# A graph-network kernel: the last 23 supertiles' messages are kept in DRAM, three slot tables serve in turn, and the turning of messages, the first fills and the last bins are done differently

## The chip, the cores and the metric

The kernel runs on one core of a Trainium2 chip. The metric is the device time of one execution in microseconds (us). The kernel before took 4111.01 us (median of three runs, 4106.05 to 4113.0).

## The reference

A message-passing layer over 12,500 nodes (128 features each) and 400,000 edges sorted by `dst`:

```python
h = jnp.maximum(_layernorm(x, axis=-1), 0.0)
# layer: f_ij = edge_attr_20 (400000 x 20), rcut = edge_weight, idx_i = src (random), idx_j = dst (sorted)
h = h @ W_in2f.T
Wij = smu(f_ij @ W_f1.T + b_f1) @ W_f2.T + b_f2
Wij = Wij * rcut_ij[:, None]
x_ij = h[idx_j] * Wij
agg = jax.ops.segment_sum(x_ij, idx_i, num_segments=h.shape[0])
out = smu(agg @ W_o1.T + b_o1) @ W_o2.T + b_o2
return x + out
```

`smu` is a smooth leaky unit; the kernel builds it from a Gelu and a linear part.

## The kernel before

**Tiles.** A tile is 128 edges. There are 3125 tiles; four make a group (782 groups), eight make a supertile (391, the last one short). The nodes fall into 98 bins of 128.

**One group.** Because `dst` is sorted, the rows of `h` that a group needs lie in one window of 42 rows. For each group the kernel makes on TensorE (PE), VectorE (DVE) and ScalarE (ACT): `hide` (L563, first filter product `pu`), `bend` (L571, Gelu), `smooth` (L579, DVE), `weigh` (L616, second product `pw`), `gather` (L597, one-hot product that picks the rows of `h`), `take` (L605), `mix` (L626, DVE: product with the rows of `h`, giving `mt`), `turn` (L636: `mt` becomes rows by edge and is multiplied by `w_o1` in the same four fp32 matmuls), `send` (L643, L646: ACT scales the rows by the edge weight into a buffer `ms`, six of which exist, with the place within the bin in column 128). Beside that, `bins`, `count`, `read` and `number` (L497, L511 to L514, L541, L550) give each edge a slot in its bin.

**The scatter.** Since `src` is random, `send` does not add. It issues, on GpSimd's (POOL's) queue, one indirect DMA for each tile (L649) that writes 128 rows of 129 floats to their slots in a table in DRAM.

**Epochs.** The edges are cut into nine epochs of 59, 59, 59, 59, 48, 37, 27, 27 and 16 supertiles (`PARTS`). Each has a table `buf` of its own with `CAP` slots a bin (768 down to 256, so Q = 6, 6, 6, 6, 5, 4, 3, 3, 2 blocks of 128). Slots that may stay empty are zeroed first (`clear`, on SP's queue). While epoch k is computed, the table of epoch k-1 is read back (`fetch`, L680, SP's queue, chunks of up to 12 blocks) and summed: `choose` (L691, DVE) makes one-hot selections `se` from column 128, `add` (L704, PE) does one matmul for each bin and block, and DVE adds four bins at a time into `agg` (L715, L717). `chores` of that kind start four groups after an epoch's first (`WAIT`).

**Order.** PE, DVE, ACT and SP run the order in which the program issues (`manual_schedule`); the main loop over `g` writes it out by hand and reaches up to three groups ahead.

**The ends.** Before the first scatter DVE converts the first indices (L305, `whole_bins`) and builds constants while POOL fills buffers with memsets (L291, L404). After the last scatter the table of the last epoch is summed and the output is made in 26 units of up to four bins: Gelu (L994, ACT), `sm` (L1000, POOL), product with `w_o2` (L264, PE), addition of the old rows of `x` (L268, DVE), store (L270). The old rows get the output bias on POOL (L250, `with_bias`), 12 of the 26 units' rows while the last epoch is scattered.

Of the kernel before, what the change touches and what calls it, by code (L numbers as in the profile page):

```python
# [19 lines left out]
P = 128  # L20
# [11 lines left out]
PARTS = (59, 59, 59, 59, 48, 37, 27, 27, 16)  # L32
# [8 lines left out]
def gnn_kernel(  # L41
# [46 lines left out]
    for a, n in eps_of:  # L88
        mean = n * SUP * P * P / N
        dev = SIGMA * math.sqrt(mean)  # L90
        CAP.append(math.ceil((mean + dev) / P) * P)
        ZMIN.append(max(0, math.floor((mean - dev) / ZP) * ZP))
# [10 lines left out]
    bufs = [dram.tile([NB * CAP[k], ROW], F32, name=f"buf{k}") for k in range(EPOCHS)]  # L103
# [24 lines left out]
    nc.vector.tensor_scalar(lift, ident, BIG, None, op0=ALU.mult)  # L128
    nc.vector.scalar_tensor_tensor(tri, irow, pcol, lift, op0=ALU.is_gt, op1=ALU.add)
    ones_h = const.tile([P, P], F16, name="ones_h")  # L130
    nc.vector.memset(ones_h, 1.0)
    rest_h = const.tile([P, P], F16, name="rest_h")
    nc.vector.tensor_sub(rest_h, ones_h, tri)
    none = const.tile([P, NB], F16, name="none")
    nc.vector.memset(none, 0.0)
# [6 lines left out]
    b1w = const.tile([P, P], F32, name="b1w")  # L142
# [14 lines left out]
    b2row = const.tile([1, P], F32, name="b2row")  # L157
    b1 = const.tile([P, 1], F32, name="b1")
    bz = const.tile([P, 1], F32, name="bz")
    w_o1 = const.tile([P, P], F32, name="w_o1")  # L160
# [4 lines left out]
    zero = const.tile([ZP, CB * max(c - z for c, z in zip(CAP, ZMIN)) * ROW // ZP], F32, name="zero")  # L165
# [69 lines left out]
    units = [(b, n, P) for b, n in chunks(NB - 1, GRP)] + [(NB - 1, 1, LASTB)]  # L235
# [39 lines left out]
    with tc.tile_pool(name="ld", bufs=4) as ld, \  # L275
# [8 lines left out]
        irow_ps = ps1.tile([P, GRP * P], F32, name="irow_ps")[:, 0:P]  # L284
        nc.vector.tensor_copy(irow_ps, irow)
# [106 lines left out]
        fill(0, nc.vector)  # L392
        nc.gpsimd.memset(w_f1, 0.0)
        nc.gpsimd.dma_start(w_f1[0:R, :], w_f1_t)
        nc.gpsimd.dma_start(w_f1[R:R + 1, :], b_f1)
        nc.sync.dma_start(fbufs[0][0:R, :], f_t[:, 0:SUP * P])
        nc.scalar.dma_start(w_o1, w_o1_t)
        nc.scalar.dma_start(x_sb[:, 1:HEAD, :], bin_rows(x, 1, HEAD - 1))
        nc.gpsimd.dma_start(w_f2, w_f2_t)
        nc.gpsimd.dma_start(b2, b_f2.rearrange("o p -> p o"))  # L400
        one["fetched"]()
        nc.gpsimd.dma_start(w_sb[:, 0:CH], w_col[:, 0:CH])
        fill(1, nc.gpsimd)
        nc.gpsimd.memset(zero, 0.0)  # L404
        clear(0, len(cleans) - 1, nc.gpsimd)
        fill(2, nc.gpsimd)
        zr = edge.tile([P, 3 * D], BF, name="zr", bufs=1)
        nc.gpsimd.memset(zr, 0.0)
        nc.gpsimd.dma_start(h_dram[NB * P:N + P, :], zr[:N + P - NB * P, :])
        fill(3, nc.gpsimd)  # L410
        nc.gpsimd.memset(x_sb[:, NB - 1, :], 0.0)
# [11 lines left out]
        def last_loads():  # L423
            nc.sync.dma_start(b2row, b_f2)
            nc.sync.dma_start(bo2, b_o2.to_broadcast([P, P]))

        groups = [(t0 + a, g) for t0, nt in sups for a, g in chunks(nt, GRP)]
        epoch = [k for k, (a, n) in enumerate(eps_of) for _ in range(n)]
# [3 lines left out]
        def load(s):  # L432
            if s >= NS:
                return
            t0, nt = sups[s]
            e0, n = t0 * P, nt * P
            fb = fbufs[s % NF]
            if s > 0:
                nc.sync.dma_start(fb[0:R, :n], f_t[:, e0:e0 + n])
            loaded[s] = (fb,)  # L440
            if s > 2:
                targets(s)

        def targets(s):
# [3 lines left out]
            rb = ld.tile([P, SUP * P], BF, name="rbc")  # L448
# [28 lines left out]

        def tiles_of(k):
# [3 lines left out]
        def bins(g):  # L482
# [5 lines left out]
            so = cnt.tile([P, GRP, NB], F16, name="so")  # L488
            if g in first:
                k = first[g]  # L490
                m = FEW if g == 0 else tiles_of(k)
                begins[k] = (t, cnt.tile([P, max(n for _, n in eps_of) * SUP], F32, name="hic", bufs=2))
                nc.vector.tensor_scalar(begins[k][1][:, :m], hi_f[:, t:t + m], float(CAP[k]), -BIG, op0=ALU.mult, op1=ALU.add)
                last[0] = none
            before = last[0]
# [3 lines left out]
            last[0] = so[:, n - 1]  # L499
# [44 lines left out]
        def number(g):  # L544
# [4 lines left out]
            ix = cnt.tile([P, GRP], I32, name="ix", bufs=8)  # L549
# [80 lines left out]
        def turn(g):  # L630
# [4 lines left out]
            for j in range(n):  # L635
                nc.tensor.matmul(pt[:, j, :], mt[:, j * P:(j + 1) * P], w_o1, start=True, stop=True)  # L636
            mixed[g] = pt

        def send(g):
# [3 lines left out]
            nc.scalar.activation(ms[:, :n, P], lo_b[:, t:t + n], AF.Copy)  # L643
            pt = mixed.pop(g)
            for j in range(n):
                nc.scalar.activation(ms[:, j, 0:P], pt[:, j], AF.Copy, scale=w_sb[:, t + j:t + j + 1])  # L646
            k, ix = epoch[g // PER], taken.pop(g)
# [36 lines left out]
        def choose(k, c):  # L684

            if c is None:
# [4 lines left out]
            nc.vector.tensor_tensor(se[:, :m], irow_ps.unsqueeze(1).to_broadcast([P, m, P]),  # L691
                                    rows_in[c][:, :m, P:P + 1].to_broadcast([P, m, P]), op=ALU.is_equal)
            sel[c] = se

        def add(k, b, q):

            g = b % GRP
            c, i = b // SPAN[k], b % SPAN[k]
            if q == 0 and g == 0:
# [11 lines left out]
            if g == GRP - 1 or b == NB - 1:  # L711
# [4 lines left out]
                else:  # L716
                    nc.vector.tensor_add(dst, dst, src)  # L717

# [15 lines left out]
        def homes():  # L734
            spent = eps_of[-1][0] * SUP // (GRP * P) * (GRP * P)
            for t in (w_sb, hi_f):
                for o in range(0, spent, GRP * P):
                    yield t[:, o:o + GRP * P]
            for o in range(0, spent // 2 // (GRP * P) * (GRP * P), GRP * P):
                yield lo_w.bitcast(F32)[:, o:o + GRP * P]  # L740

        held = {unit: home.rearrange("p (b d) -> p b d", b=GRP)
                for unit, home in zip([u for u in units if u[1] == GRP][::2], homes())}
        ahead = list(held)
# [26 lines left out]
        stats(edge, 0)  # L771
        few = edge.tile([FEW, P], BF, name="few", bufs=1)
# [3 lines left out]
        deviations(0, 1)  # L776
# [16 lines left out]
        product()  # L793
        bins(0)
        for s in (1, 2):
            load(s)
# [12 lines left out]
        for s in (1, 2):  # L809
            targets(s)  # L810
# [19 lines left out]
        def output_bias():  # L830

            nc.vector.tensor_scalar(w_o2, w_o2, GC, None, op0=ALU.mult)
            nc.vector.tensor_scalar(bz, b1, ZS, None, op0=ALU.mult)
            nc.vector.tensor_scalar(b1w, onesb, b1, LIN, op0=ALU.mult, op1=ALU.mult)
            pb1 = bank("pb1")[:, 0, :]
            nc.tensor.matmul(pb1, b1w, w_o2, start=True, stop=True)
# [64 lines left out]
        for g in range(NG):  # L901
            s = g // PER
            k = epoch[s]
            g0, ng = eps_of[k][0] * PER, min(eps_of[k][1] * PER, NG - eps_of[k][0] * PER)
            i = g - g0
            if g == (FEW // SUP - 3) * PER:
                assert not opening
            if g % PER == 0:
                load(s + 3)
# [7 lines left out]
            elif k + 1 < EPOCHS:  # L917
# [5 lines left out]
            if k and i == 0:  # L923
                work = [(b, q) for b in range(NB) for q in range(Q[k - 1])]
# [5 lines left out]
            if k and k == EPOCHS - 1 and i >= WAIT and ahead:  # L930
                unit = ahead.pop(0)
                old_rows(unit, held[unit], nc.sync)
            lo = hi = 0
# [4 lines left out]
            if g:  # L938
# [3 lines left out]
            number(g + 1)  # L942
            weigh(g + 1)
            gather(g + 1)
            take(g + 1)
            parts(k - 1, lo + (hi - lo) // 2)
            mix(g + 1)
            step()
            hide(g + 2)
            bend(g + 2)  # L950
            count(g + 2)
            smooth(g + 2)
            if g % PER == 0:
                pick((g + 4) // PER)
            bins(g + 3)
# [238 lines left out]
```

## Time and profile before

| What | us |
|---|---|
| median of three runs | 4111.01 |
| profiled execution, its own time | 4114.52 |
| span of its trace | 4112.7 |
| busy: PE, DVE, POOL, ACT | 3675.1, 3450.5, 3096.4, 1944.9 |
| first and last scatter start (L649) | 19.9, 4022.2 |
| mean granted TensorE clock | 0.976 |

The span runs from the first instruction to the last; 1.8 us of the execution's own time lie outside it. Shares of busy time are averages over the whole span. A matmul's busy time overlaps that of the next. "Idle before" names what ended an engine's wait; "issue" means that the profile shows nothing that it waited for.

### The profile page before, as it was taken

What the parts mean: (1) busy time and instruction counts of PE and PEld (TensorE: products, weight loads), DVE (VectorE), ACT (ScalarE), POOL (GpSimd) and SP (SyncE); (2) the same over time, 40 slices, a digit from 0 to 9 for tenths busy, and PEclk for the clock granted to TensorE, in tenths of its full rate; (3) what the DMA queues carried; (4) which work ended last, traced back from release to release, by engine and by line L of the source; (5) the groups of instructions that cost most, each with busy time, mean ns of one, the idle gap of its engine ahead of it and who ended that gap; (6) DMA issues with size and microseconds to landing.
All of it is one profiled execution on the core that took longest, in us unless ns stands there. A gap on an engine that the chain in (4) does not pass through costs nothing.

```text
span 4112.7 us, 74065 instructions
## 1 busy us (share of the span) xinstructions
PE 3675.1 (89%) x21113; PEld 2552.3 (62%) x21117; DVE 3450.5 (84%) x7657; ACT 1944.9 (47%) x5690; POOL 3096.4 (75%) x3199
## 2 busy tenths in 40 slices
PE   7878887999888998979999979999899989999898
PEld 4445545666655666646666656666677767666678
DVE  8988776888878888868888868888799979888897
ACT  4457754444444444435444434444444434444442
POOL 6777777777777777777777777777777777777775
PEclk9999998999999999989999989999999999999999
DMA  6866656766647666646766647777688789887668
GB/s 187 231 187 182 191 166 183 213 202 195 188 141 219 198 201 197 199 146 196 212 199 187 199 148 207 210 204 211 176 228 223 195 230 242 221 228 221 176 195 248
DMA packets 564245, 820.83 MB, mean 200 GB/s; under 512 B 178033, under 2 KB 378488, under 8 KB 563698
## 3 DMA queue, kind: packets, MB, share of 16 engines
q1 hardware_dynamic: 456096, 604.98, 53.5%
q0 software_dynamic: 100320, 207.40, 15.7%
q10 hardware_dynamic: 7410, 3.65, 0.3%
q8 instruction: 167, 2.74, 0.3%
q14 instruction: 252, 2.06, 0.2%
HBM read 442.34 MB, written 373.37 MB: 198 GB/s over the span
## 4 chain that ended last, share of the span: by engine, by line
PE 39%; DVE 29%; DMA 18%; ACT 6%; issue 5%; POOL 2%; DVEq 0%; ACTq 0%; POOLq 0%; SPq 0%
DMA buf<-ms,ix 17%; PE pt L636 11%; PE pg L704 9%; PE pw L616 8%; DVE se L691 8%; PE pu L563 7%; DVE mt L626 5%; DVE so L497 5%; DVE sm L579 3%; DVE sl L541 3%; ACT ge L571 2%; ACT ms L646 2%; PE ph L597 2%; POOL buf L649 2%; DVE agg L717 1%
## 5 line engine op out<-in xcount | busy, mean ns | idle before, releaser
L649 POOL DMA_INDIRECT buf<-ms,ix x3125 | 3025.4, 968 | 972.7 <-issue 395.9
L646 ACT ACTIVATE ms<-pt,w_sb 128x128 f32<-128x128 f32 x3125 | 888.8, 368 | 1125.5 <-PE pt L636 1118.0
L636 PE MATMUL pt<-w_o,mt 128*128 128x128 f32 x6250 | 881.3, 284 | 390.9 <-DVE mt L626 388.4
L704 PEld LDWEIGHTS pg<-se,rw 128*128 128x128 f32 x8036 | 1052.4, 192 | 249.7 <-issue 210.8
L704 PE MATMUL pg<-se,rw 128*128 128x128 f32 x8036 | 1148.8, 280 | 4.5 <-DVE se L691 3.7
L636 PEld LDWEIGHTS pt<-w_o,mt 128*128 128x128 f32 x6250 | 765.5, 193 | 478.7 <-DVE mt L626 474.5
L497 DVE SCALAR_TENSOR_TENSOR so<-irow_ps,hi_f,so 128x98 f16<-128x98 f32 x3116 | 989.0, 317 | 82.7
L616 PE MATMUL pw<-sm,w_f 128*128 128x512 f32 x1564 | 826.7, 611 | 10.4 <-DVE sm L579 8.5
L563 PE MATMUL pu<-f,w_f 128*128 128x512 f32 x1564 | 811.4, 601 | 0.0
L626 DVE SCALAR_TENSOR_TENSOR mt<-pw,b,hg 128x512 f32<-128x512 f32 x782 | 583.6, 746 | 207.3 <-ACT hg L605 203.8
L571 ACT ACTIVATE ge<-pu 128x512 f32<-128x512 f32 x782 | 468.6, 599 | 532.7 <-PE pu L563 526.5
L579 DVE SCALAR_TENSOR_TENSOR sm<-pu,ge 128x512 f32<-128x512 f32 x782 | 535.3, 684 | 187.8 <-ACT ge L571 182.0
L691 DVE TENSOR_TENSOR se<-irow_ps,rw 128x1536 f32<-128x1536 f32 (+1 forms) x345 | 587.9, 1704 | 114.3 <-DMA rw<-buf 110.2
L605 ACT ACTIVATE hg<-ph 128x512 f32<-128x512 f32 x782 | 468.6, 599 | 62.1 <-PE ph L597 44.9
L541 DVE TENSOR_REDUCE sl<-pc 128x4 f32<-128x392 f32 x782 | 434.7, 556 | 0.0
L643 ACT ACTIVATE ms<-lo_b 128x4 f32<-128x4 bf16 x782 | 159.9, 204 | 358.7 <-DMA buf<-ms,ix 358.2
L597 PE MATMUL ph<-oh,hw 126*128 126x512 bf16 x770 | 298.3, 387 | 0.0
L563 PEld LDWEIGHTS pu<-f,w_f 128*128 128x128 f32 x1564 | 253.5, 196 | 53.4 <-issue 43.8
L511 PE MATMUL pc<-so,tri 128*128 128x392 f16 x782 | 257.9, 330 | 1.0 <-DVE sl L541 0.8
L616 PEld LDWEIGHTS pw<-sm,w_f 128*128 128x128 f32 x1564 | 241.1, 195 | 24.7 <-DVE sm L579 21.4
L513 PEld LDWEIGHTS <-rest_h 128*128 128x128 f16 x781 | 76.5, 98 | 265.9 <-issue 265.9
L513 PE MATMUL pc<-so,rest_h 128*128 128x294 f16 x781 | 225.1, 288 | 0.0
(161 smaller groups left out, 1391.0 us busy)
## 6 DMA issues: line engine op xcount, KB each, us to landing
rw<-buf SPq DMA_DIRECT2D x292, 774.0 KB
rbc<-rel_dram SPq DMA_DIRECT2D x389, 256.0 KB
buf<-zero SPq DMA_DIRECT2D x243, 387.0 KB
buf<-ms,ix POOLq DMA_INDIRECT x3125
buf<-zero SPq DMA_DIRECT2D x193, 258.0 KB
rw<-buf SPq DMA_DIRECT2D x49, 645.0 KB
f<-in_f_t SPq DMA_DIRECT2D x390, 80.0 KB
hw<-h_dram SPq DMA_DIRECT2D x770, 31.5 KB
```

The lines of the kernel that those rows point to most:

```text
L497: nc.vector.scalar_tensor_tensor(so[:, j], irow_ps[:, :NB], hi_f[:, t + j:t + j + 1], so[:, j - 1] if j else before, op0=ALU.is_equal, op1 ...
L541: nc.vector.tensor_reduce(sl[:, :n], pc[:, :n], op=ALU.max, axis=AX.X)
L563: nc.tensor.matmul(pu[:, :n], w_f1, loaded[g // PER][0][:, o:o + n], start=True, stop=True)
L571: nc.scalar.activation(ge[:, :n], units_of[g][:, :n], AF.Gelu, scale=ZS)
L579: nc.vector.scalar_tensor_tensor(sm[:, :n], units_of.pop(g)[:, :n], LIN, hidden[g][:, :n], op0=ALU.mult, op1=ALU.add)
L616: nc.tensor.matmul(pw[:, :n], w_f2, hidden.pop(g)[:, :n], start=True, stop=True)
L626: nc.vector.scalar_tensor_tensor(mt[:, :n], pws.pop(g)[:, :n], b2, rows_of.pop(g)[:, :n], op0=ALU.add, op1=ALU.mult)
L636: nc.tensor.matmul(pt[:, j, :], mt[:, j * P:(j + 1) * P], w_o1, start=True, stop=True)
L646: nc.scalar.activation(ms[:, j, 0:P], pt[:, j], AF.Copy, scale=w_sb[:, t + j:t + j + 1])
L649: i = nc.gpsimd.indirect_dma_start(out=bufs[k][:, :], out_offset=bass.IndirectOffsetOnAxis(ap=ix[:, j:j + 1], axis=0), in_=ms[:, j, :], in ...
L691: nc.vector.tensor_tensor(se[:, :m], irow_ps.unsqueeze(1).to_broadcast([P, m, P]), rows_in[c][:, :m, P:P + 1].to_broadcast([P, m, P]), op= ...
L704: nc.tensor.matmul(pgs[0][:, g, :], rows_in[c][:, o, 0:P], sel[c][:, o, :], start=(q == 0), stop=(q == Q[k] - 1))
```

## The change

Seven things are done:

1. **Ten epochs instead of nine**, with 59, 59, 59, 59, 48, 37, 27, 20, 16 and 7 supertiles; Q of the last ones is 3, 3, 2, 1. The sum of Q over all epochs goes from 41 to 42.
2. **The last two epochs (23 supertiles, from `EARLY` = 368) are computed early.** After supertile 67, 76, 85 and so on to 265 (every ninth in epochs 1 to 4) one of them is put in between: 6, 7, 6 and 4 of them in the four epochs. Their messages aren't scattered then, but written to `kept_rows` in DRAM by one DMA a group on ACT's queue; their slots are kept in `ix_kept`. After the main loop `refill` reads each group back on SP's queue, four groups ahead, and `scatter` puts it into its table.
3. **Three tables serve in turn** (`BUFS`), so only epochs 0 to 2 are cleared. A later user of a table adds 128 or more to column 128 (`mark`), and `choose` compares with a row of `irow` shifted as much (`marks`), so that what an earlier epoch left there isn't selected.
4. **`turn` transposes** (matmul with `ident` in transpose mode) for the first 368 supertiles; `w_o1` is applied once to `agg`, by 25 matmuls of up to 512 columns (`fold`), after epoch 7 has been summed. The 23 others keep the old form.
5. **POOL's first fills** come after five two-column memsets that DVE does behind the first four sums of `bins(0)`, and DVE's counting constants (`tri`, `rest_h` and others) move to just ahead of `bins(0)`. Five small loads go from POOL's queue to SP's.
6. **The bias** is added to the old rows on DVE, while the kept messages are scattered; the rows are loaded then too, into buffers that are free by that time.
7. **At the end** the first full selection of the last epoch is made in pieces of four blocks, and one output unit of four bins is cut into two of two.

```diff
-PARTS = (59, 59, 59, 59, 48, 37, 27, 27, 16)
+PARTS = (59, 59, 59, 59, 48, 37, 27, 20, 16, 7)
+SENT_LAST = 2
+BUFS = 3
...
-    bufs = [dram.tile([NB * CAP[k], ROW], F32, name=f"buf{k}") for k in range(EPOCHS)]
+    stores = [dram.tile([NB * CAP[k], ROW], F32, name=f"buf{k}") for k in range(min(BUFS, EPOCHS))]
+    bufs = [stores[k % BUFS][0:NB * CAP[k], :] for k in range(EPOCHS)]
...
+        def quiet_ends():
+            for t in (zero, fbufs[2], zr, fbufs[3], x_sb[:, NB - 1, :]):
+                nc.vector.memset(t[:, 0:2], 0.0)
+            nc.gpsimd.memset(zero, 0.0)
+            clear(0, len(cleans) - 1, nc.gpsimd)
+            fill(2, nc.gpsimd)
...
+        flow, rest_of = [], list(range(EARLY, NS))
+        start, gap = eps_of[1][0], (eps_of[5][0] - eps_of[1][0]) // (NS - EARLY)
+        for s in range(EARLY):
+            flow.append(s)
+            if s >= start and (s - start) % gap == gap - 1 and rest_of:
+                flow.append(rest_of.pop(0))
...
             for j in range(n):
-                nc.tensor.matmul(pt[:, j, :], mt[:, j * P:(j + 1) * P], w_o1, start=True, stop=True)
+                if s_of(g) < EARLY:
+                    nc.tensor.transpose(pt[:, j, :], mt[:, j * P:(j + 1) * P], ident)
+                else:
+                    nc.tensor.matmul(pt[:, j, :], mt[:, j * P:(j + 1) * P], w_o1, start=True, stop=True)
...
+            m = epoch[s_of(g)] // BUFS
+            if m:
+                nc.scalar.activation(ms[:, :n, P], lo_b[:, t:t + n], AF.Identity, bias=mark[:, m:m + 1])
...
+            if s_of(g) >= EARLY:
+                nc.scalar.dma_start(kept_rows[:, t - kept_tile:t - kept_tile + n, :], ms[:, :n, :])
+                return
+            scatter(g, ms)
...
-            nc.vector.tensor_tensor(se[:, :m], irow_ps.unsqueeze(1).to_broadcast([P, m, P]),
-                                    rows_in[c][:, :m, P:P + 1].to_broadcast([P, m, P]), op=ALU.is_equal)
+            own = marks[:, k // BUFS * P:(k // BUFS + 1) * P]
+            first = k == EPOCHS - 1 and c == order_of[k][1]
+            for a, n in chunks(m, GRP if first else m):
+                nc.vector.tensor_tensor(se[:, a:a + n], own.unsqueeze(1).to_broadcast([P, n, P]),
+                                        rows_in[c][:, a:a + n, P:P + 1].to_broadcast([P, n, P]), op=ALU.is_equal)
...
+        def fold():
+            dst = plain.pop(0)
+            w = dst.shape[1]
+            po = ps1.tile([P, GRP * P], F32, name=("pu", "ph")[len(folded) % 2])
+            nc.tensor.matmul(po[:, :w], w_o1, dst, start=True, stop=True)
+            nc.scalar.activation(dst, po[:, :w], AF.Copy)
+            folded.append(w)
...
-            elif k + 1 < EPOCHS:
+            elif k + 1 < BUFS:
...
+        def refill(g):
+            if g < NG:
+                t, n = groups[g]
+                back[g] = msg.tile([P, GRP, ROW], F32, name="ms")
+                nc.sync.dma_start(back[g][:, :n, :], kept_rows[:, t - kept_tile:t - kept_tile + n, :])
+
+        g1 = EARLY * PER
+        for g in range(g1, g1 + 4):
+            refill(g)
+        for g in range(g1, NG):
+            refill(g + 4)
+            k = chores(g)
+            scatter(g, back.pop(g))
+            parts(k - 1, hi)
+            if g - g1 >= 2:
+                old(g - g1 - 2)
+            biased(g - g1 - 10)
...
-                with_bias(unit, xr, nc.gpsimd)
+                with_bias(*rows_got[n], nc.vector)
```

In the main loop `g` now runs along `seq`, the groups in the order of `flow`; the look-ahead (`number`, `weigh`, `mix`, `hide`, `bins` and the rest) follows that order too, and the `chores` are done at the groups of the first 368 supertiles alone.

More of the change, by code (lines that the diff above doesn't have):

```diff
@@ L698, in add @@
             c, i = b // SPAN[k], b % SPAN[k]
+            halved = k == EPOCHS - 1 and b // GRP == whole // GRP - 1
+            if halved:
+                g %= GRP // 2
             if q == 0 and g == 0:
@@ L929, in gnn_kernel @@
                 choose(k - 1, 0)
[L930 to L933, printed above, removed]
+            lo = hi = done
             if k and i >= WAIT:
```

238 lines of the change are left out of this document (142 added, 96 removed).

## The prediction

> **What bounds the kernel now.** I read the page first: busy shares, then the costliest groups. PE and DVE look like the bound.
>
> ```profile
> PE 3675.1 (89%) x21113; PEld 2552.3 (62%) x21117; DVE 3450.5 (84%) x7657; ACT 1944.9 (47%) x5690; POOL 3096.4 (75%) x3199
> ```
>
> Next I read the scatter's line (L649) and the timeline in the middle of the span. In the first line stand minimum, median and maximum of one scatter in ns, then the first and last start.
>
> ```profile
> L649 POOL DMA_INDIRECT buf<-ms,ix x3125: 956/962/1460, 19.9 to 4022.2; - x196
> ...
> 2003.14 0.96 POOL L649 DMA_INDIRECT buf<-ms,ix  x1 [0.30 <-ACT ms L646]
> 2004.40 0.96 POOL L649 DMA_INDIRECT buf<-ms,ix  x1 [0.30 <-issue]
> 2005.67 0.96 POOL L649 DMA_INDIRECT buf<-ms,ix  x1 [0.30 <-issue]
> ```
>
> Scatters start 1.266 us apart whatever "released" them: 0.96 busy and always the same 0.30 idle. The 3124 distances at 1.266 make 3955.0 us; first to last start is 4002.25. So POOL's queue is the bound from 19.9 to 4022.2, and all other waiting inside comes to 47.3 us. The waits say the same:
>
> ```profile
> ACT ms L643 <- DMA buf<-ms,ix: 358.2, 163, 6.2
> DVE se L691 <- DMA rw<-buf: 110.2, 9, 20.5
> ```
>
> ACT waits 358 us for a message buffer to be scattered: computing is ahead of POOL. The second wait is the epoch's turn: DVE stands still until POOL has caught up. The profiled run is thus 19.9 (head) + 3955.0 + 47.3 (stalls) + 90.5 (from the last scatter's start to the end, 4112.7) + 1.8 outside the span = 4114.5, which is 3.5 above the median of the runs. The change scatters the same 3125 tiles, so only head, stalls and tail can give anything.
>
> By the Trainium skill (Perfetto Trace Analysis, Identifying the Most-Contended Engine) the engine with the highest occupancy is the one to work on, with LDWEIGHTS busy share in place of matmul's for TensorE; here that is DVE at 84%, and POOL at 75% would have room. The steady 1.266 us speaks against it: POOL's idle quarter is mostly the 0.30 us between scatters. What follows if the occupancy is right is the first rival.
>
> **Head.** The timeline of the first 20 us:
>
> ```profile
> 3.90 5.12 DVE L305 CAST ssf<-ss 128x48 f32<-128x48 int32 x1
> ...
> 4.62 0.97 POOL L291 MEMSET f<- 128x1024 f32 x1
> ...
> 7.99 0.97 POOL L291 MEMSET f<- 128x1024 f32 x1
> ...
> 19.93 1.04 POOL L649 DMA_INDIRECT buf<-ms,ix  x1 [10.27 <-ACT ms L646]
> ```
>
> A cast of 48 columns takes 5.1 us and ends when POOL's last memset of a buffer does; the same line's casts of 512 columns take 0.50. DVE then works without a break to `so`, so the chain gets 4.9 us shorter. Put into it: the constants (five instructions of 0.10 to 0.37, starting about 0.9 us in all) and five marks of about 0.06. First scatter: 19.9 - 4.9 + 0.9 + 0.3 = 16.2. POOL's fills, 4.4 us of them, now run beside the second half of the chain and end at about 15.3; if one of DVE's operations there is held as the cast was, the head is 20 again. Bounds 15 to 20. The loads moved to SP's queue cost nothing while they land before DVE uses them at about 6 us (0.4 us an issue, six ahead of `w_f2`); the 4 us gained is the cover.
>
> The skill (SBUF — State Buffer, Who interferes with whom) says why: a DVE cast in a two-port mode and a POOL operation lock each other out for a whole instruction, and operations from PSUM or with two inputs don't contend with a POOL fill. The cast's 5.12 against 0.50 agrees, and by it nothing in the second half is held.
>
> **PE.** A transpose of this shape is one matmul instruction; the product with `w_o1` is two.
>
> ```profile
> 472.40 0.60 PE L211 MATMUL pg<-ident,rw 128*128 128x128 f32 x4
> ...
> 2005.47 1.06 PE L636 MATMUL pt<-w_o,mt 128*128 128x128 f32 x8
> ```
>
> Four take 0.60, eight 1.06; without the last one's 0.275 that is 0.11 us an instruction either way. So 0.45 us a group leave PE, 330 us over 736 groups. On the path that is worth nothing by itself. It pays for the next step. `fold` adds 25 x 0.86 = 22 us of PE, while PE has only sums to do.
>
> **Early supertiles.** Each put-in supertile is two groups for which POOL gets no work, so the compute engines must have earned that time. After the boundaries at 624, 1223 and 1822 us, when nothing holds them, the starts of Gelu (L571) are 4.73 us apart over 30 groups: 4.35 in the groups without a selection, where PE is the last to be ready (DVE waits 0.40 for `hg` and 0.56 for `ge`), 5.2 to 6.0 in those with one (L691, 1.75 us), where DVE is. Transposes shorten the first kind only, about half of the groups: 4.73 - 0.5 x 0.45 = 4.5. POOL takes 4 x 1.266 = 5.06 a group. Eighteen groups earn 18 x 0.56 = 10.1 us; the put-in pair costs 2 x 3.7 = 7.4 (3.6 to 4.0 is the distance at the end of epoch 0, where there are no sums either). So epochs 1 to 3 hold, with 19 pairs: after a boundary the messages are 4 us ahead, and the nearest pair comes three supertiles later (4 + 6 x 0.56 = 7.4). In epoch 4 the sums are denser (distance 5.0 after 2423 us, PE at 4.6 to 4.8; with transposes 4.75): 18 x 0.31 = 5.6 against 7.4 for four pairs, the first after two supertiles (5.3 against 7.4): 2.1 + 3 x 1.8 = 7 us of stall. Bounds 0 and 25. Epoch 7 has 294 sums in 36 groups; DVE needs about 4.9 a group there, just under POOL's pace.
>
> **Tables in turn.** Table k is reused three epochs on, read out one epoch on: no wait. 46 messages' writes of 264 KB (one issue of about 0.4 us on ACT, which is 47% busy: nothing) and as many reads come in, some 90 MB of zeroing (L179, 387 KB each) goes out: DMA, at 0.6 to 0.8 busy, is relieved. The indirect DMAs stay 3125.
>
> **The last 181 scatters.** `refill` stands on SP's queue behind reads of rows (L680) that wait for matmuls, and POOL waits for `refill`. Six buffers are 30 us of POOL's work, four reads of 774 KB took 9 us at the last boundary: covered, 0 to 10 us, I take 2. The bias adds on POOL go: a scatter distance with one in it is 2.43 us, with two 3.65, so 12 of them cost 14.2. On DVE they are 26 x 0.68 = 18 us in the 229 us of these scatters, in which DVE has only selections and sums of two epochs to do (42 chunks of 1.75 and 50 sums of 0.68, 108 us): nothing. Epoch 8's 196 sums (0.224 each on PE, 44 us) have 67 us and end about with the last scatter, as the 36 left over do now. Stalls: 47.3 - 14.2 + 7 + 2 = 42.1.
>
> **Tail.** Lines of the timeline: last scatter, first and last whole sum of the last epoch.
>
> ```profile
> 4022.18 0.96 POOL L649 DMA_INDIRECT buf<-ms,ix  x1 [0.30 <-issue]
> ...
> 4036.85 0.69 DVE L717 TENSOR_TENSOR agg<-agg,pg 128x512 f32<-128x512 f32 x1 [1.31 <-PE pg L704]
> ...
> 4102.02 0.69 DVE L717 TENSOR_TENSOR agg<-agg,pg 128x512 f32<-128x512 f32 x1 [1.09 <-PE pg L704]
> ```
>
> 14.7 us to the first, 65.2 for 23 more (2.83 each), 10.7 to the end. PE bounds the middle part: 24 instructions of 0.112 a unit, 2.69. With Q = 1 it is 16: 1.79. DVE has 0.6 + 0.6 and a third of a selection, 1.76 by starts. Then the round from a sum to the product with `w_o2` is next: sum 0.69, Gelu 0.72, POOL's `sm` 1.27 and what stands before the sum on DVE, up to 1.75, against one and a half units. Between 1.8 and 2.6 a unit; I take 2.2, since two engines at 1.8 will now and then wait for that round: 50.6. The first sum stays at 14.7 (SP waits 4.1 for the landing, and chunks of 774 KB again lead), the end at 10.7 less 1.5 for halved units. Tail 74.5; bounds 65 to 84.
>
> **Sum.** 16.2 + 3955.0 + 42.1 + 74.5 + 1.8 = 4089.6 in a run like the profiled one, 24.9 less than it; taken from the median, 4086.
>
> **Rivals.**
>
> *PE or DVE is the bound (2%).* Then 338 us of matmuls (2944 x 0.115) less 22 for `fold` come off: about 3800. For it: the shares. Against it: the constant 1.266.
>
> *POOL starves (slower, 11%).* If transposes don't shorten the distance (DVE, at 4.2 busy a group, sets it: 4.73, and 5.0 in epoch 4) and a put-in group costs 5.0 like the others, because it carries an extra DMA on ACT's queue and its loads, a pair costs 10.0 against 6.1 earned in 18 groups: 19 x 3.9 + 4 x 8.9 = 110, less 16 for the four starts: 4170 to 4175. It decides from where 18 x (5.06 - distance) falls below the pair's cost. For it: DVE's 84%. Against it: 3.6 us groups exist.
>
> *Half of that, or a blocked SP queue (11%).* Distance 4.73 but pairs at 3.7: 19 x 1.3 + 4 x 6.2 - 16 = 33 us instead of 7, 4112; or refills 20 us late instead of 2: 4104. That is no change.
>
> *Below the sum (4%).* 1.8 us a unit in the tail (-9), no stall in epoch 4 (-7), no late refill (-2): 4068; and if the faster PE also takes the 12 us that the first 125 scatters lose now: 4056.
>
> Forecast 72%, from 4060 to 4103. The range takes in the bounds (head -1 and +4, stalls -9 and +18, tail -9 and +10, not all at once) and the third rival: 4060 to 4120. A change within 0.2% (8 us) can't be told from none: faster 0.78, same 0.11, slower 0.11.
>
> **What would show it.** Right: scatters at 1.266 throughout, first at about 16, last at 4010 to 4020; the cast at 0.2; the changed kernel's L683 with one instruction a tile; no POOL gap over 5 us at the put-in pairs of epochs 1 to 3, small ones in epoch 4; last-epoch sums 2.2 apart. Wrong: POOL gaps of 3 to 8 us after each put-in pair, scatters further apart than 1.266 among the last 181, or a DVE operation of several us beside POOL's fills.

## The result, and the profile after

The changed kernel took 4083.48 us (median of five runs, 4078.92 to 4087.04) beside 4108.48 us for the kernel before: a ratio of 0.9939, 95% interval 0.9924 to 0.9953, 25.0 us less. Run again later (second profile below) it had 4088.18 beside 4109.72, ratio 0.9947 (0.9934 to 0.9961).

The busy shares of the changed kernel's page look as they did before: PE lost 169 us, and POOL still stands at 75%.

```profile
PE 3506.1 (86%) x18417; PEld 2254.1 (55%) x18420; DVE 3472.7 (85%) x7739; ACT 2036.5 (50%) x5716; POOL 3047.7 (75%) x3168
```

The scatter's line, now L710 (minimum, median, maximum in ns, then first and last start), for the two kinds of message:

```profile
L710 POOL DMA_INDIRECT buf<-ms,ix x2944: 952/958/1442, 19.6 to 3777.3; - x197
L710 POOL DMA_INDIRECT buf<-ms,ix_kept x181: 954/958/1474, 3778.6 to 4007.7; - x181
```

The last start is at 4007.7, 14.5 us earlier. The first is at 19.6, where 16.2 had been predicted. The median distance of starts is 1.263 us. In the kernel before it was 1.266, and that looks like a gain of the change (3124 x 0.003 = 9.4 us), but it is none: the second profile of the same changed kernel has 1.266.

```profile
L710 POOL DMA_INDIRECT buf<-ms,ix x2944: 955/962/1474, 19.3 to 3786.3; - x197
L710 POOL DMA_INDIRECT buf<-ms,ix_kept x181: 955/962/1450, 3787.6 to 4017.7; - x181
```

So the second profile (4088.9 us) is the one to lay beside the predicted sum, which was made at 1.266:

| Term (us) | before | predicted | second profile | first profile |
|---|---|---|---|---|
| first scatter | 19.9 | 16.2 | 19.3 | 19.6 |
| 3124 distances | 3955.0 | 3955.0 | 3955.0 | 3945.6 |
| stalls between scatters | 47.3 | 42.1 | 43.3 | 42.5 |
| last scatter to end | 90.5 | 74.5 | 69.4 | 69.5 |
| outside the span | 1.8 | 1.8 | 1.8 | 1.8 |
| sum, before rounding its terms | 4114.5 | 4089.6 | 4088.9 | 4078.9 |

The sum came out within 1 us by luck: the first scatter is 3.1 us later than predicted and the tail 5.1 us shorter, and the stalls are 1.2 us longer, so the errors nearly cancel. The tail alone makes 21 of the 25.7 us between the profiles of the kernel before and the second one. The stalls are right by another split: in the first profile 16.7 of the 42.5 us lie in epoch 4, where 7 had been predicted on top of the 1.5 of before. The timeline of POOL at the first put-in supertile of epoch 4 (first profile):

```profile
2454.85 0.96 POOL L710 DMA_INDIRECT buf<-ms,ix  x1 [0.30 <-ACT ge L617]
2460.49 0.96 POOL L710 DMA_INDIRECT buf<-ms,ix  x1 [4.68 <-ACT ms L699]
2463.56 0.96 POOL L710 DMA_INDIRECT buf<-ms,ix  x1 [2.12 <-ACT ms L694]
```

POOL has nothing to send for 4.7 and then 2.1 us. At the other three pairs of epoch 4 the starts are 4.36, 5.21 and 3.50 us apart. In epochs 1 to 3 only two distances exceed 1.9 us (2.78 and 2.23). Among the 181 kept messages no distance exceeds 1.8 us.

The head of the changed kernel, its first message and its first scatter:

```profile
5.00 0.18 DVE L318 CAST ssf<-ss 128x48 f32<-128x48 int32 x1
...
13.02 0.76 POOL L185 DMA_DIRECT2D buf<-zero  x1
...
15.66 1.14 ACT L699 ACTIVATE ms<-pt,w_sb 128x128 f32<-128x128 f32 x4 [2.21 <-PE pt L683]
...
19.59 1.04 POOL L710 DMA_INDIRECT buf<-ms,ix  x1 [3.77 <-DVE so L540]
```

The cast takes 0.18 us, and the first tile's message is there at 16.0, which fits the predicted 16.2. The scatter starts 3.6 us later; the releaser named (`so`, ended long before) can't be it. What had moved is L185, the clear of the last bin, from 7.1 to 13.0.

The tail, in the timeline of the first profile: the last scatter, the first and the last whole sum.

```profile
4007.72 0.95 POOL L710 DMA_INDIRECT buf<-ms,ix_kept  x1 [0.30 <-issue]
...
4022.10 0.68 DVE L784 TENSOR_TENSOR agg<-agg,pg 128x512 f32<-128x512 f32 x1
...
4063.22 0.69 DVE L784 TENSOR_TENSOR agg<-agg,pg 128x512 f32<-128x512 f32 x1 [0.20 <-PE pg L771]
```

14.4 us to the first sum, 41.1 for 22 more (1.87 each), 14.0 for the two halves and the end.

### The profile page after: what moved, and what is told of

The parts are those of the page before. It is cut to its first block, busy times and chain, and to the rows that moved or that the text cites. A ratio compares the mean times of both kernels' runs of the same rounds, so it can differ in the third digit from the quotient of the medians.

```text
span 4077.2 us, 68671 instructions
## 1 busy us (share of the span) xinstructions
PE 3506.1 (86%) x18417; PEld 2254.1 (55%) x18420; DVE 3472.7 (85%) x7739; ACT 2036.5 (50%) x5716; POOL 3047.7 (75%) x3168
## 3 DMA queue, kind: packets, MB, share of 16 engines
q14 instruction: 253, 2.07, 0.2%
## 4 chain that ended last, share of the span: by engine, by line
PE 37%; DVE 36%; DMA 13%; ACT 5%; issue 5%; POOL 3%; DVEq 0%; ACTq 0%; SPq 0%; POOLq 0%
PE pw L662 11%; DVE se L755 11%; DMA buf<-ms,ix 10%; PE pg L771 8%; PE pu L609 7%; PE pt L683 6%; DVE mt L672 6%; DVE so L540 5%; DVE sl L584 4%; DVE sm L625 4%; POOL buf L710 3%; ACT ge L617 3%; PE ph L643 2%; DMA rw<-buf 2%; DVE oh L507 2%
## 5 line engine op out<-in xcount | busy, mean ns | idle before, releaser
L710 POOL DMA_INDIRECT buf<-ms,ix x2944 | 2835.4, 963 | 927.0 <-issue 367.7
L771 PEld LDWEIGHTS pg<-se,rw 128*128 128x128 f32 x8232 | 1084.8, 195 | 333.9 <-issue 270.3
L771 PE MATMUL pg<-se,rw 128*128 128x128 f32 x8232 | 1179.3, 283 | 87.7 <-DVE se L755 70.2
L540 DVE SCALAR_TENSOR_TENSOR so<-irow_ps,hi_f,so 128x98 f16<-128x98 f32 x2936 | 929.8, 317 | 78.0
L662 PE MATMUL pw<-sm,w_f 128*128 128x512 f32 x1564 | 886.2, 649 | 44.4 <-DVE sm L625 41.6
L683 PE MATMUL pt<-ident,mt 128*128 128x128 f32 x2944 | 469.9, 283 | 374.0 <-DVE mt L672 371.6
L755 DVE TENSOR_TENSOR se<-irow_ps,rw 128x1536 f32<-128x1536 f32 (+2 forms) x356 | 602.3, 1692 | 189.5 <-DMA rw<-buf 185.9
L683 PEld LDWEIGHTS pt<-ident,mt 128*128 128x128 f32 x2944 | 328.2, 142 | 458.2 <-DVE mt L672 455.0
L554 PE MATMUL pc<-so,tri 128*128 128x392 f16 x736 | 243.4, 331 | 2.8 <-DVE agg L423 1.7
L710 POOL DMA_INDIRECT buf<-ms,ix_kept x181 | 175.2, 968 | 55.2 <-issue 54.3
```

Source lines behind the costliest of these rows:

```text
L540: nc.vector.scalar_tensor_tensor(so[:, j], irow_ps[:, :NB], hi_f[:, t + j:t + j + 1], so[:, j - 1] if j else before, op0=ALU.is_equal, op1 ...
L662: nc.tensor.matmul(pw[:, :n], w_f2, hidden.pop(g)[:, :n], start=True, stop=True)
L683: nc.tensor.transpose(pt[:, j, :], mt[:, j * P:(j + 1) * P], ident)
L710: i = nc.gpsimd.indirect_dma_start(out=bufs[k][:, :], out_offset=bass.IndirectOffsetOnAxis(ap=ix[:, j:j + 1], axis=0), in_=ms[:, j, :], in ...
L755: nc.vector.tensor_tensor(se[:, a:a + n], own.unsqueeze(1).to_broadcast([P, n, P]), rows_in[c][:, a:a + n, P:P + 1].to_broadcast([P, n, P] ...
L771: nc.tensor.matmul(pgs[0][:, g, :], rows_in[c][:, o, 0:P], sel[c][:, o, :], start=(q == 0), stop=(q == Q[k] - 1))
```

## Experiments

**Transposes alone.** The kernel before, with `turn` transposing in epochs 0 to 7 and `fold` while the last epoch is computed:

```diff
-                nc.tensor.matmul(pt[:, j, :], mt[...], w_o1, start=True, stop=True)
+                if epoch[g // PER] < EPOCHS - 1:
+                    nc.tensor.transpose(pt[:, j, :], mt[...], ident)
+                else:
+                    nc.tensor.matmul(pt[:, j, :], mt[...], w_o1, start=True, stop=True)
...
+                if k == EPOCHS - 2:
+                    plain.append(dst)
+                    if len(plain) > 1:
+                        fold()
```

> The kernel before with the transposes alone: turn transposes in epochs 0 to 7, the last epoch keeps w_o1, and the sums are multiplied by w_o1 in 25 matmuls while the last epoch is computed. If POOL's scatter queue is the bound: about 300 us of matmuls leave PE and the time stays within 0.2% of the kernel before (ratio 0.998 to 1.002); scatters stay 1.26 to 1.27 apart, the stalls between them stay at 40 to 50 us, and ACT's wait for message buffers (358 us before) grows by 100 to 300 us. If PE or DVE is the bound: about 300 us less, ratio 0.93.

4115.12 against 4103.40 us, ratio 1.0033 (1.0021 to 1.0045): slower. The page, the scatter's line and the wait for message buffers (total, times, longest):

```profile
PE 3486.4 (85%) x18167; PEld 2219.8 (54%) x18167; DVE 3430.4 (83%) x7657; ACT 1982.4 (48%) x5715; POOL 3079.6 (75%) x3199
```

```profile
L652 POOL DMA_INDIRECT buf<-ms,ix x3125: 952/958/1428, 19.6 to 4015.6; - x196
```

```profile
ACT ms L646 <- DMA buf<-ms,ix: 632.5, 285, 6.5
```

PE is 189 us less busy than before and the kernel is no faster. ACT's wait for POOL grew by 274 us (358 before). That settles the bound: POOL's queue, not PE. That it is even slower was not expected. In its profile the stalls between scatters are 50.5 us, 3.2 more than before, and the tail is 97.9 us, 7.4 more. Within the stalls 26.8 us lie in the last 125 scatters, against 14.6 before: 25 folds come in the last epoch, where the groups are mostly 5.2 us or more apart already. What makes the tail longer no run shows. In the changed kernel the same folds come when nothing is computed any more, and no scatter waits.

**The changed kernel without transposes.** `turn` keeps the product with `w_o1` everywhere, and `fold` goes.

```diff
-                if s_of(g) < EARLY:
-                    nc.tensor.transpose(pt[:, j, :], mt[:, j * P:(j + 1) * P], ident)
-                else:
+                if True:
                     nc.tensor.matmul(pt[:, j, :], mt[:, j * P:(j + 1) * P], w_o1, start=True, stop=True)
...
-                if k == EPOCHS - SENT_LAST - 1:
+                if False:
                     plain.append(dst)
```

> The changed kernel with the products by w_o1 kept in all supertiles and no fold. If the transposes pay for the put-in supertiles, as predicted: the distance of groups is 4.7 instead of 4.5 and the stalls between scatters grow from 42 to 65 to 85 us, spread over the 23 pairs of epochs 1 to 4, worst in epoch 4; time 20 to 40 us above the changed kernel, about the kernel before's (ratio 0.999 to 1.004 to the kernel before). If DVE sets the distance and the transposes bring nothing: stalls stay at 42, ratio 0.994. If PE is the bound: 300 us more, ratio 1.07.

4149.16 us, ratio to the kernel before 1.0111 (1.0096 to 1.0127). Stalls are 112.2 us, 70 more than in the changed kernel; at 21 of the 23 pairs starts are now 2.5 to 8.6 us apart. The direction was as expected, the size was not. So transposes do pay for the put-in supertiles; without them the change would be a loss of 1.1%. What they save shows in PE's timeline. First this kernel, in a group without a selection:

```profile
654.65 1.06 PE L683 MATMUL pt<-w_o,mt 128*128 128x128 f32 x8
655.54 1.02 PE L662 MATMUL pw<-sm,w_f 128*128 128x512 f32 x2
656.40 0.38 PE L643 MATMUL ph<-oh,hw 126*128 126x512 bf16 x1
```

A group of that kind in the changed kernel:

```profile
665.03 0.60 PE L683 MATMUL pt<-ident,mt 128*128 128x128 f32 x4
665.53 1.13 PE L662 MATMUL pw<-sm,w_f 128*128 128x512 f32 x2
666.50 0.38 PE L643 MATMUL ph<-oh,hw 126*128 126x512 bf16 x1
```

From start to start, eight instructions take 0.89 us and four transposes 0.50, which saves 0.39. But the product behind them goes from 0.86 to 0.97. Net 0.28, and such groups come 4.06 us apart instead of 4.35, both by the starts of Gelu.

The Gelu starts of both kernels give the price list that the prediction had estimated. The loop makes the Gelu of a group two groups ahead, so a pair's price is counted two groups behind it, over the stretch in which the pair is turned and sent. (By the pair's own Gelu starts it would be 9.2 and the ordinary group 4.56; the 20 groups together, which decide, come out the same within 0.3 us.) POOL takes 4 x 1.263 = 5.05 us a group.

| us | predicted | changed kernel | without transposes |
|---|---|---|---|
| ordinary group, epochs 1 to 3 | 4.5 | 4.60 | 4.75 |
| ordinary group, epoch 4 | 4.75 | 4.79 | 4.95 |
| put-in pair, epochs 1 to 3 | 7.4 | 8.7 | 8.9 |
| put-in pair, epoch 4 | 7.4 | 8.8 | 9.1 |

In the changed kernel's epochs 1 to 3, 18 groups earn 18 x 0.45 = 8.1 against 8.7: 0.6 short at each pair, which the head start of each epoch covers. In epoch 4 they earn 18 x 0.26 = 4.7 against 8.8, so 4.1 are missing, 16.4 for four pairs; measured 15.5 above the normal distance. Without transposes 18 x 0.30 = 5.4 against 8.9, so 3.5 are missing from the first pair on.

**A put-in supertile after every seventh.** All 23 then lie in epochs 1 to 3.

```diff
-        start, gap = eps_of[1][0], (eps_of[5][0] - eps_of[1][0]) // (NS - EARLY)
+        start, gap = eps_of[1][0], (eps_of[4][0] - eps_of[1][0]) // (NS - EARLY)
```

> The changed kernel with a put-in supertile after every seventh instead of every ninth, so all 23 lie in epochs 1 to 3 and none in epoch 4. By the predicted price list (a group earns 0.56 us, a pair costs 7.4): 14 groups earn 7.8, so no stalls in epochs 1 to 3 and none in epoch 4, about 16 us less stall than the changed kernel's 42.5. By what the kernel without transposes and the changed one show together (group 4.71 less about 0.15, so 16 groups take 73 us and POOL's 14 take 70.7): 1.5 to 3 us lost at each pair after the first few of an epoch, 20 to 40 us in epochs 1 to 3, and the sum no better than the changed kernel.

4100.73 us in one run, 13 and 17 more than the changed kernel's two medians; its span is 21.8 us longer than the first profile's, both with scatters 1.263 apart. Stalls are 65.2 us: epoch 4 is clean, but nearly every pair in epochs 1 to 3 has a distance of 2.8 to 4.6 us. 14 groups earn 6.4 against 8.6. The predicted list (7.8 against 7.4) falls and the measured one holds. Every ninth was just sparse enough.

**The four supertiles of epoch 4 moved.** Two to the end of epoch 0 and two to the end of epoch 5, where the turn of the epoch leaves DVE standing for 20 us.

```diff
-            if s >= start and (s - start) % gap == gap - 1 and rest_of:
-                flow.append(rest_of.pop(0))
-        flow += rest_of
+            if start <= s < eps_of[4][0] and (s - start) % gap == gap - 1:
+                flow.append(rest_of.pop(0))
+            if s in (start - 1, eps_of[6][0] - 1):
+                flow += [rest_of.pop(0) for _ in range(2)]
...
```

> The changed kernel with the four put-in supertiles of epoch 4 moved: two to the end of epoch 0 and two to the end of epoch 5, where DVE stands still for 20.6 and 20.7 us at the turn of the epoch. If a pair stalls the scatters only where 18 groups don't earn its 7.4 us: the four gaps of 3.5 to 8.7 us in epoch 4 vanish, no new ones come, DVE's waits at those two turns shrink to 5 to 8 us, stalls fall from 42.5 to 24 to 28, time 14 to 18 us under the changed kernel (ratio to the kernel before 0.988 to 0.991). If a pair stalls the scatters wherever it stands (its message buffers, its DMA on ACT's queue): gaps of 3 to 6 us come at the new places, ratio 0.993 to 0.995.

4063.85 us against 4106.30 for the kernel before, ratio 0.9899 (0.9882 to 0.9915). Stalls are 27.6 us, no distance in epoch 4 exceeds 1.9 us, and none came at the new places.

```profile
L712 POOL DMA_INDIRECT buf<-ms,ix x2944: 952/958/1440, 19.9 to 3762.9; - x197
L712 POOL DMA_INDIRECT buf<-ms,ix_kept x181: 954/958/1327, 3764.1 to 3993.1; - x181
```

The last scatter starts 14.6 us earlier than in the first profile of the changed kernel. DVE's waits for rows at the two turns shrank to 0.33 us each, further than the expected 5 to 8; a pair that costs 8.7 and not 7.4 explains part of that. At the turn from epoch 4 to 5, which has no pairs ahead of it any more, the wait grew from 9.0 to 19.8 us.

**The bias on DVE alone.** The kernel before, with the 12 adds of the last epoch moved from POOL to DVE.

```diff
+            if k == EPOCHS - 1 and i >= WAIT + 8 and asked:
+                unit = asked.pop(0)
+                with_bias(unit, held[unit], nc.vector)
...
-                with_bias(unit, xr, nc.gpsimd)
+                if unit not in held:
+                    with_bias(unit, xr, nc.gpsimd)
```

> The kernel before with one edit: the bias of the 12 units whose old rows are loaded during the last epoch is added on DVE there, not on POOL between scatters. If each such add holds the scatters up for 1.2 us: no scatter distance of 2.43 or 3.65 is left among the last 125, the stalls there fall from 14.6 to under 3 us, and the time falls by 12 to 14 us (ratio 0.9967). If DVE, which has 4.9 of 5.06 us busy a group there, is what is late next: stalls of several us near the end instead, ratio 0.999 to 1.001.

4102.19 us, ratio 0.9994 (0.9985 to 1.0003): no change can be seen. The adds are gone from between the scatters, but the stalls of the last 125 only fall from 14.6 to 11.1 us. In this profile the tail is 3.4 us longer (93.9 us), and the granted TensorE clock there is 0.61 from 4070.8 to 4078.8 (1.00 at the same sums in the kernel before), so the tail's part of the account is not settled. POOL's timeline, where before an add stood:

```profile
3932.62 0.96 POOL L649 DMA_INDIRECT buf<-ms,ix  x1 [0.30 <-issue]
3935.11 0.96 POOL L649 DMA_INDIRECT buf<-ms,ix  x1 [1.53 <-ACT ms L646]
...
3938.90 0.96 POOL L649 DMA_INDIRECT buf<-ms,ix  x1 [0.31 <-issue]
3942.60 0.96 POOL L649 DMA_INDIRECT buf<-ms,ix  x1 [2.74 <-ACT hg L605]
```

POOL now waits for the messages instead. After the first six groups of that epoch all but the last come 5.24 us or more apart (Gelu starts, median 5.47) against POOL's 5.05. Three quarters of the time of the adds had filled a wait that was there anyway. The rival expectation was right.

**Ten epochs alone.** The kernel before, with the last epochs 27, 20, 16 and 7 and nothing computed early.

```diff
-PARTS = (59, 59, 59, 59, 48, 37, 27, 27, 16)
+PARTS = (59, 59, 59, 59, 48, 37, 27, 20, 16, 7)
```

> The kernel before with ten epochs (27, 20, 16, 7 at the end) but nothing computed early. Tail 90 to about 70 us as in the changed kernel (from last scatter start to the end). If the dense sums of the last epochs hold the messages up: 160 sums in the 10 groups of the last epoch make 3.6 us a group more for PE, 8 against POOL's 5.06, so POOL stands still for 15 to 40 us there, and the gain of the tail is lost: ratio 0.998 to 1.006. If six message buffers and the order hide that: ratio 0.995.

4111.90 us, ratio 1.0020 (1.0010 to 1.0029): a little slower. The last 250 scatters lose 32.7 us against 16.4 before, and the tail is 81.1 us instead of 90.5. In the changed kernel, with the last two epochs computed early, they lose 2.6. So early computing is what lets a short last epoch pay. But the tail is 11.6 us longer than the changed kernel's, which has the same Q = 1: a unit takes 2.31 us by the starts of its sums (not 2.5, as the next expectation has it from one chunk) against 1.87. Something else in the change shortens it.

**Ten epochs, without the bias of the late rows.** One candidate is POOL, which in the tail does a bias add between its `sm` operations. This kernel leaves these adds out, so its output lacks the bias there; it serves for timing alone.

```diff
-                with_bias(unit, xr, nc.gpsimd)
+                if unit in held:
+                    with_bias(unit, xr, nc.gpsimd)
```

> The kernel before with ten epochs, and the bias left out for the units whose old rows are loaded after the main loop (their outputs lack the bias), so that no bias add of POOL stands between its sm operations at the end. With ten epochs alone the tail is 81.1 us, 11.6 longer than the changed kernel's 69.5, at about 2.5 us a unit instead of 1.9, and POOL makes 1.27 us of sm and 1.27 us of bias there. If POOL's bias adds set that pace: 1.9 to 2.0 us a unit and a tail of 68 to 73 us. If the late loads of the old rows or the missing pieces set it: 79 to 82 again.

The tail is 80.8 us and a unit 2.30: not POOL's adds. (The time, 4119.12 us in one run, comes from scatters 1.266 apart.) ACT's queue in the tail of this kernel, with DVE's sum (L717) and its last reading of `hg` (L268) ahead of it:

```profile
4059.33 0.68 DVE L717 TENSOR_TENSOR agg<-agg,pg 128x512 f32<-128x512 f32 x1
...
4060.87 0.69 DVE L268 TENSOR_TENSOR ms<-pu,hg 128x512 f32<-128x512 f32 x1 [0.86 <-PE pu L264]
...
4061.60 0.47 ACTq L244 DMA_DIRECT2D hg<-in_x  x1
4062.11 1.34 ACT L995 ACTIVATE ge<-agg,bz 128x512 f32<-128x512 f32 x2 [4.14 <-DVE ms L268]
```

The Gelu's sum was ready at 4060.0. It starts at 4062.1, behind a load of old rows on ACT's own queue, which waits until DVE (`ms`, L268, to 4061.6) has read the buffer `hg`. In the kernel with ten epochs alone seven such loads stand 4.60 to 4.89 us apart from 4052.8 on, each right ahead of two Gelus, so they set about 2.35 us a unit:

```profile
4062.29 0.47 ACTq L244 DMA_DIRECT2D hg<-in_x  x1
4062.80 1.33 ACT L994 ACTIVATE ge<-agg,bz 128x512 f32<-128x512 f32 x2 [3.28 <-POOL hg L250]
```

The changed kernel loads all old rows ahead of the tail, and there ACT waits for DVE's sum alone:

```profile
4042.90 0.72 ACT L1117 ACTIVATE ge<-agg,bz 128x512 f32<-128x512 f32 x1 [0.82 <-DVE agg L784]
```

**The changed kernel without its seventh part.** The first selection whole, no halved unit.

```diff
-            first = k == EPOCHS - 1 and c == order_of[k][1]
+            first = False
...
-    units = [(b, n, P) for b, n in chunks(whole - GRP, GRP)]
-    units += [(whole - GRP, GRP // 2, P), (whole - GRP // 2, GRP // 2, P)]
+    units = [(b, n, P) for b, n in chunks(whole, GRP)]
...
```

> The changed kernel without the seventh part: the first full selection of the last epoch whole, the unit of four bins not cut. Predicted worth of the halved units: 1.5 us at the end; of the selection in pieces: nothing, since the first sum comes at 14.4 us after the last scatter's start in the changed kernel and 14.7 in the kernel before. So the tail from the last scatter's start to the end of the span is 70 to 72 us instead of 69.5. If the pieces carry the gain of the first sums: 73 to 75.

4080.19 us in one run; the tail is 68.5 us, not 70 to 72: 14.7 to the first sum, 42.9 for 23 more (1.87 each), 10.9 to the end. Part 7 is worth nothing that shows: five of the other kernels here that have it, with the same last epochs, have tails of 67.3 to 68.5 us. This leaves the loading ahead as the likely cause of the other 11.6 us; it was found by exclusion and by the lines above, and wasn't run alone.

**An early clear, by DVE and POOL.** In the changed kernel `zero` is filled by DVE before `irow_ps` is made, and POOL issues the clear right after.

```diff
+        nc.vector.memset(zero, 0.0)
         nc.vector.tensor_copy(irow_ps, irow)
         nc.gpsimd.memset(w_f1, 0.0)
+        clear(0, len(cleans) - 1, nc.gpsimd)
...
-            nc.gpsimd.memset(zero, 0.0)
-            clear(0, len(cleans) - 1, nc.gpsimd)
```

> The changed kernel with the buffer of zeros filled by DVE at the start and the last bin's clear issued by POOL then, not at 13.0 us. If the first scatter waits for that clear's landing: it starts at 16.0 to 16.5 us instead of 19.6, and the span is about 3 us shorter unless the next messages are late. If it waits for something else that ends at 18.7: still 19 to 20.

4075.88 us in one run.

```profile
17.76 1.14 ACT L699 ACTIVATE ms<-pt,w_sb 128x128 f32<-128x128 f32 x4 [3.50 <-PE pt L683]
18.42 1.04 POOL L710 DMA_INDIRECT buf<-ms,ix  x1 [3.22 <-ACT ms L699]
```

The first scatter now follows its own message at once, so the late clear had held it. (The landing of the clear is in no view; that the scatter waited for it is inferred from what the edit moved.) But the start, 18.4, is neither the 16.0 to 16.5 nor the 19 to 20 expected, since the message itself is 2.1 us later. DVE's fill puts 0.8 us into the chain, and the product `pw` took 1.96 us instead of 1.12. The granted TensorE clock was 0.54 during it and 1.00 in the first profile, so this part need not come from the edit. The fifth scatter, 24.80 in the first profile, came at 26.14, and the 126th at 185.3 instead of 185.4: the gain is gone by then. That the span is 3.1 us shorter comes from later stages.

**Both edits, beside the changed kernel.** The moved supertiles, and `zero` filled by POOL itself at 1.7 us, where it stands idle. The other lines of the two edits are as above.

```diff
         nc.gpsimd.memset(w_f1, 0.0)
+        nc.gpsimd.memset(zero, 0.0)
+        clear(0, len(cleans) - 1, nc.gpsimd)
...
+            if s in (start - 1, eps_of[6][0] - 1):
+                flow += [rest_of.pop(0) for _ in range(2)]
```

> The changed kernel with two edits: the four put-in supertiles of epoch 4 at the ends of epochs 0 and 5, and the buffer of zeros filled and the last bin's clear issued by POOL right at the start, where it stands idle from 1.7 us on, instead of behind DVE's first sums. If POOL's fill at the start holds nothing up: first message at 15.7 and first scatter at 16 to 16.5 us instead of 19.6; but the fifth scatter, the second group's, comes at 24.8 in the changed kernel with and 26.1 without the wait, so of these 3.4 us some 1 to 2.5 stay. Stalls 24 to 30 from scatter to scatter with the wait for the second group in it, no gap over 3 us in epoch 4; time 15 to 19 us under the changed kernel run beside it (ratio to the kernel before 0.988 to 0.991). If POOL's fill holds DVE's first operations, as the four fills held the cast in the kernel before: first scatter at 18 to 20 again, and only the 15 us of the moved supertiles.

> The changed kernel unaltered, beside the version with both edits on the same chip: ratio to the kernel before 0.992 to 0.996, four gaps of 3.5 to 8.7 us in epoch 4 and the first scatter at 19 to 20 us as in its first profile, scatters 1.263 apart as in the kernels run since.

4071.11 us against 4088.18 for the changed kernel on the same chip, 17.1 less; ratios to the kernel before 0.9910 (0.9895 to 0.9925) and 0.9947 (0.9934 to 0.9961). This beats both kernels. In the second profile of the changed kernel the scatters are 1.266 apart, not the expected 1.263; the rest is as expected. With both edits the first scatter is at 17.6, but the next gaps grew, and the 126th is at 186.2. So the early clear adds nothing that shows, and the moved supertiles alone explain the gain. How far the opening varies by itself shows in PE's timeline of the changed kernel, first and second profile, each with the view of that stretch behind it (the last three figures of it are the granted clock, the DMA share and GB/s):

```profile
12.93 1.12 PE L662 MATMUL pw<-sm,w_f 128*128 128x512 f32 x2 [0.21 <-DVE sm L625]
...
12.93:14.05 1.12, 1.12 (x2) 0.29 (x2) 0.58 (x2) 0.52 (x2) 1.12 (x3) 1.00 0.39 117
```

```profile
12.94 2.07 PE L662 MATMUL pw<-sm,w_f 128*128 128x512 f32 x2 [0.21 <-DVE sm L625]
...
12.94:15.01 2.07, 2.07 (x2) 0.49 (x2) 0.58 (x2) 0.52 (x2) 2.07 (x4) 0.50 0.49 132
```

## Why the prediction was right, and where its steps failed

- **The bound.** Right, and shown: taking 189 us of busy time off PE alone made the kernel no faster, and DVE's waits for rows grew from 110 to 140 us. The Trainium skill's rule (Perfetto Trace Analysis, Identifying the Most-Contended Engine) points to the engine with the highest occupancy, DVE before and after. The runs disagree: with DVE's busy time as it was (3474.8 us against 3472.7), moving four supertiles made the span 16.8 us shorter.
- **Head: failed.** In the first profile the chain got shorter as worked out (cast 0.18, message at 16.0). The step that failed is "POOL's fills ... now run beside the second half of the chain": their time was counted, but not that the clear behind them is a DMA for which the first scatter waits. That cost 3.4 of the 3.7 us. In the second profile the message was there only at 17.5, at half the clock, and the scatter started at 19.3. The first scatter was also the wrong mark: the 126th starts at 184.3 to 187.9 us in four kernels with the new opening, and at 186.5 and 187.4 in two with the old one (all with scatters 1.263 apart), so what the new opening brings is about 1 us, less than it varies by itself. The Trainium skill's rule (SBUF — State Buffer, Who interferes with whom) held in the changed kernel: none of DVE's operations beside the moved fills took longer than 0.8 us. In the kernel before, the trace goes further than the rule, which speaks of one whole instruction: the cast lasted from 3.90 to 9.02 us, over five memsets of POOL between 4.62 and 8.96.
- **Transposes: mis-sized.** 0.45 us a group predicted, 0.28 measured: four transposes save 0.39, and the product behind them takes 0.11 longer.
- **Pair price: mis-sized, and the main error.** 7.4 predicted, 8.7 to 8.8 measured. The 3.6 to 4.0 us groups at the end of epoch 0 were the wrong row: there they come behind groups of 8.9 and 5.7 us, and the last 14 groups of that epoch are 5.03 us apart in the mean, which is POOL's pace. The put-in groups come 4.3 us apart. The plan held in epochs 1 to 3 by a hair. In epoch 4 the price explains 4 x 1.4 of the 8.5 us by which the 7 fell short, and the ordinary group (4.79 for 4.75) another 4 x 0.7. (A slip beside it: at 4.73 a group, as in two of the rivals, 18 groups earn 6.0 us and not 6.1.)
- **Bias adds: the price was right, the reason was not.** In the changed kernel the stall of 14.2 is gone, but there nothing is computed in that stretch any more either. On the kernel before, where the messages are late too, the same edit took away 3.5 us of stalls and no time that shows.
- **Kept messages and tables in turn.** No stall; the 2 us taken for late reads weren't needed. The folds were free only because they come there. The three tables were not run alone; no wait shows that they cause.
- **Tail: 5 us too long, and for the wrong reason.** The failed term is the 2.2 us a unit, put down to the round from a sum to the product with `w_o2`; 1.87 was measured. Q = 1 brings 9.4 us by itself (90.5 to 81.1), at 2.31 a unit. The loads of old rows on ACT's queue, which the prediction's tail left out, are the likely other 11.6. The 1.5 us for halved units are not there.

## What to carry to other kernels

When one queue sets the pace, price work for the other engines by what they have to spare between its steps, with every price from the stage where the work will stand; a few tenths of a us a group decided between a gain of 0.6% and a loss of 1.1%. Put extra work where the other engines stand still anyway, here the turn of an epoch. Before a stall is booked as a gain, ask what is late behind it: of three stalls taken away here (the cast, the bias adds, the clear) each let another wait take its place.

## What the runs showed of the hardware that was not expected

- The distance of indirect DMAs on POOL's queue belongs to the execution. It was 1.263 us in one run of the changed kernel and 1.266 in another, 9.4 us over 3124; and on the chip of the second profile (1.266) the kernel with both edits had 1.263. What sets it is not known.
- The two-instruction fp32 product of 128x128 by 128x512 took 1.12 us right behind four fp32 transposes (median of 711 in the first profile), and 1.02 behind the fp32 products with `w_o1` (median of 46 in the same run).
- In the opening the same product, started at the same 12.93 us, took 1.12 us in one execution and 2.07 in another. The granted clock was 1.00 in the first and 0.50 in the second, where it had been 1.00 up to about 12.7 us and was again from about 19.6. The Trainium skill (TensorE: Matmul & The Clock Gate, Part 1: The HAM clock gate) has the clock halved after an idle window of some 3.4 us, and has these windows run free of the kernel's start. The 6.9 us at half clock agree with two such windows; which stretch counted as idle no run here shows.
